# Directional scans as four 48x48 products in the quarters of TensorE's array instead of one 96x96 product

## The chip, the cores and the metric

The kernel runs on one core of a Trainium2 chip. The metric is the device time of one execution in microseconds. All data are fp32.

## The reference, cut to what matters

The input `x` is (4, 48, 256, 256): 4 images, 48 channels. Four layers each add to `x` a function of its group norm (16 groups of 3 channels). Layers 0 and 3 are gated feed-forward layers (1x1 convolution, 3x3 depthwise convolution, GELU gate, 8x8 block DFT with a mask). Layers 1 and 2 are the subject here: four scans over lines, each a recurrence whose step is a convolution of width 5 along the line, from 48 to 48 channels.

```python
def step(w, b):
    def f(carry, inp):
        nxt = inp + _conv1d(carry, w, b)      # 48 -> 48 channels, 5 taps along the line
        return (nxt, nxt)
    return f
# down: rows 0..255;  up: rows 255..0, input shifted by one row, same weights
# right: columns 0..255 of the result of up;  left: columns 255..0
x = x + _L1_conv_ref(_gn(x), ...)
```

A scan has 255 dependent steps. Within one step, the four images and the 256 positions of the line are independent.

## The kernel before, in words

**Stages.** `net_kernel` runs, in this order: `input_stats` (reads `x`, statistics for the first norm), `layer0`, the scans of layers 1 and 2 (`open_scans`, `scans`), `layer3`. Images are taken in two pairs `p`; layers 0 and 3 walk through strips of `RB` = 8 rows, with a hand-written order on TensorE, VectorE and ScalarE (`by_clocks`, `in_turns`).

**A scan step.** A line of a pair is a tile slice of 96 partitions: partitions 0 to 47 hold the even positions of the line, 48 to 95 the odd ones. The free dimension holds 2 images x 128 positions with a zero at each end. In this parity layout the 5 taps over 256 positions become 3 taps over 128 position pairs, with 96x96 weights in which two of the twelve 48x48 blocks are zero (`scan_weights`). `conv` (L728 to L733) issues the three products into one PSUM tile `acc`; then one VectorE instruction adds the incoming line, and the bias where it isn't folded in, and writes the new line (L811 in down, L846 in up, L885 in right, L923 in left). The next product of the pair needs this line.

```python
acc = self.ps1[p].tile([CC, 2, m], F32, name="acc")
for t in range(3):
    self.nc.tensor.matmul(acc, w[:, t, :], carry[:, :, t : t + m], start=(t == 0), stop=(t == 2))
```

**Order.** `scans` runs a generator for each pair. It takes a step of pair 0, then one of pair 1, by turns; pair 1 starts 16 steps later. TensorE and VectorE execute in the order in which the program emits (`manual_schedule`); the other engines and DMA queues are ordered by the scheduler. PSUM gives each pair two buffers of `acc`.

**Around a step**, for each group of 8 lines of a pair:

- *down*: SP loads `in` from the layer's input (L786, L795); two ScalarE ACTIVATEs (L806) apply the norm and the bias in place; after 8 steps Pool issues the write of the lines to `dn` (L818).
- *up*: SP loads `in` from `dn`; ScalarE copies the finished lines, transposed, to `blk` (L853); every fourth group a 32-row block goes to `up` (L858).
- *right*: SP loads `in` from `up`; Pool issues the write to `rt` (L889).
- *left*: SP loads `in` from `rt` (L906); every fourth group ScalarE's queue loads the residual block `blk` from the layer's input (L911), into one of three buffers that both pairs share. After a group, Pool adds the lines to the block in two instructions (L933), VectorE takes `bn_stats` of it during the second half of the next group (L946, four instructions), and the block is written to `xout` (L939).

`in` has three buffers a pair, the lines have three sets of 8. DRAM tensors between the layers keep parity and position in separate dimensions, so a load of 8 lines of `x` or `up` has contiguous runs of 4 x 16 elements, 256 B.

**Layers 0 and 3** read and write that layout too. In layer 0, `back` adds the residual in eight VectorE instructions per half strip (L463) and stores `xo` (L475). In layer 3, `normed` makes `u` from `raw` in eight ScalarE instructions per strip (L1056).

Of the kernel before, what the change touches and what calls it, by code (L numbers as in the profile page):

```python
# [9 lines left out]
F32 = mybir.dt.float32  # L10
AF = mybir.ActivationFunctionType
# [10 lines left out]
BK = 32  # L22
PW = 16
BH = BK // 2
# [7 lines left out]
class Net:  # L32
# [9 lines left out]
    def __init__(self, ctx, tc, args, out, B, H, W):  # L42
# [9 lines left out]
        self.xs = [  # L52
            dram.tile([n, C, 2, 2, self.WB, 2, H // 2, BH], F32, name=f"x{i}", tag=f"x{i}")
            for i in (1, 2, 3)
        ]
        self.dn = dram.tile([n, CC, H, W], F32, name="dn", tag="dn")
        self.up = dram.tile([n, C, 2, 2, self.HB, 2, W // 2, BH], F32, name="up", tag="up")
        self.rt = dram.tile([n, CC, W, H], F32, name="rt", tag="rt")
# [3 lines left out]
        self.grp6 = self.load("grp6", [CC, CC])  # L62


        self.inv1 = self.load("inv1", [128, 64])
        self.fwd1_p = self.load("fwd1_p", [128, 64])

        self.fwd1 = self.load("fwd1", [128, 64])
        self.inv1_p = self.load("inv1_p", [128, 64])
# [11 lines left out]
    def new_stats(self, halves=False, rows=CC):  # L81


        n = self.B if halves else self.NP
        t = self.stat.tile([CP, n, self.NP * self.NCH // n, 6], F32, name=f"st{n}", tag="st")
        return [t[0:rows, p] for p in range(n)]

    def norm(self, stats):
        grp = self.grp if len(stats) == self.NP else self.grp6
        steps = self.norm_steps(stats, self.grp7 if stats[0].shape[0] == CP else grp)  # L90
        while True:
            try:
                next(steps)
            except StopIteration as end:
                return end.value

    def norm_steps(self, stats, grp, name=""):

        nc, n, rows = self.nc, len(stats), stats[0].shape[0]
        with self.tc.tile_pool(name="ps_n", bufs=1, space=PSUM) as psn:  # L100
# [4 lines left out]
            for p in range(n):  # L105
                nc.vector.bn_aggr(mv[:, p, :], stats[p])
                yield
            pm = psn.tile([rows, n], F32, name="pm")
# [21 lines left out]
        return [sc[:, p] for p in range(n)]  # L130

    def by_image(self, scs):

        found = []
        for p in range(self.NP):
            for b in range(2):
                t = self.stat.tile([CC, 2], F32, name=f"si{p}{b}", tag=f"si{p}{b}")
                for k in range(2):
                    self.nc.sync.dma_start(t[k * C : (k + 1) * C, :], scs[p][64 * b : 64 * b + C, :])
                found.append(t)  # L140
        return found

    def strip(self, x, p, lo, hi):

        return x[p].rearrange("c i e v f h w -> i c e (v f) h w")[:, :, :, :, lo:hi, :]
# [17 lines left out]
    def layer0(self, scs, stats):  # L163
# [7 lines left out]
        with ExitStack() as st:  # L171
# [263 lines left out]
            def back(n, z, q0):  # L435
# [6 lines left out]
                if q0 == 0:  # L442
                    state["xo"] = io.tile([CP, 2, self.WB, 2, RH, 2, 8], F32, name="xo", tag="xo")
                xo = state["xo"]
                for q0 in (q0,):
                    po = ps.tile([128, 2, 4, 2, 2, RH, 2, 4], F32, name="po", tag="w")
                    for q in range(4):
                        for l in range(2):
                            for lo, m in ((0, 64), (64, C)):
                                for o in range(2):  # L450
                                    f = slice(64 * o, 64 * o + 64)
                                    nc.tensor.matmul(
                                        po[lo : lo + m, o, q, :, :, :, l, :].rearrange("p e f h w -> p (e f h) w"),
                                        z[f, q0 // 2 + q, l, lo : lo + m], self.inv1_p[f, :],
                                        start=True, stop=True,
                                    )
                    rs = res[:, :, q0 * PW : (q0 + 8) * PW].rearrange(
                        "p (h e) (q w f) -> p e f q h w", e=2, f=2, q=8
                    )
                    for e in range(2):  # L460
                        for f in range(2):
                            for o in range(2):
                                nc.vector.tensor_tensor(  # L463
                                    xo[:, e, q0 // 2 : q0 // 2 + 4, f, :, o],
                                    po[0:CP, o, :, e, f].rearrange("p q h l w -> p q h (l w)"),
                                    rs[:, e, f, o::2], ALU.add,
                                )
                if q0 + 8 < NQ:
                    return
                flat = xo.rearrange("p e v f h l w -> p (e v f h l w)")  # L470
                for k in range(RB * W // MM):
                    nc.vector.bn_stats(stats[p][:, h0 * W // MM + k, :], flat[:, k * MM : (k + 1) * MM])
                to = self.strip(self.xs[0], p, h0 // 2, h0 // 2 + RH)
                for b in range(2):
                    nc.gpsimd.dma_start(  # L475
                        to[b].rearrange("c e v h w -> c (e v) (h w)"),
                        xo[64 * b : 64 * b + C].rearrange("p e v f h l w -> p (e v f) (h l w)"),
                    )
# [210 lines left out]
    def scan_weights(self, n, which):  # L689


        nc = self.nc
        w = self.wp1.tile([CC, 3, CC], F32, name=f"w{n}_{which}", tag=f"w_{which}")
        b = self.wp1.tile([CC, 1], F32, name=f"b{n}_{which}", tag=f"b_{which}")
        nc.gpsimd.memset(w, 0.0)
        taps = self.a[f"L{n}_{which}_w"]
        for e in range(2):
            for f in range(2):
                lo, hi = (1 if e < f else 0), (2 if e > f else 3)
                for t in range(lo, hi):  # L700
                    nc.sync.dma_start(
                        w[e * C : (e + 1) * C, t, f * C : (f + 1) * C], taps[:, 2 * t + e - f, :]
                    )
            nc.sync.dma_start(b[e * C : (e + 1) * C, :], self.a[f"L{n}_{which}_b"])
        self.scan_w[n, which] = w, b

    def open_scans(self, st):

        pool = lambda name, bufs, **k: st.enter_context(self.tc.tile_pool(name=name, bufs=bufs, **k))
        self.wp1, self.pin, self.pblk = pool("w1", 1), pool("in1", 3), pool("blk1", 3)
        self.ps1 = [pool(f"ps1_{p}", 2, space=PSUM) for p in range(self.NP)]
        self.lines, self.turn, self.scan_w = [], [0] * self.NP, {}
        for which in ("down", "right", "left"):
            self.scan_weights(1, which)
        M = self.W // 2
        assert self.H == self.W
        for p in range(self.NP):
            self.lines.append([])  # L720
            for k in range(3):
                t = self.wp1.tile([CC, RB, 2, M + 2], F32, name=f"line{p}{k}", tag=f"line{p}{k}")
                self.nc.gpsimd.memset(t[:, :, :, 0:1], 0.0)
                self.nc.gpsimd.memset(t[:, :, :, M + 1 : M + 2], 0.0)
                self.lines[p].append(t)

    def conv(self, p, w, carry):

        m = self.W // 2
        acc = self.ps1[p].tile([CC, 2, m], F32, name="acc")  # L730
        for t in range(3):
            self.nc.tensor.matmul(acc, w[:, t, :], carry[:, :, t : t + m], start=(t == 0), stop=(t == 2))  # L732
        return acc  # L733

    def scans(self, scs):


        stats = self.new_stats(halves=True)

        def pair(p, scs):  # L740
            for n in (1, 2):
                got = stats[2 * p : 2 * p + 2]
                yield from self.scan_layer(n, p, self.xs[n - 1][p], self.xs[n][p], scs, got)
                if n == 1:
                    if p == self.NP - 1:
                        self.scan_weights(2, "left")
                    scs = yield from self.norm_steps(got, self.grp6, f"p{p}")

        with self.tc.manual_schedule(engines={mybir.EngineType.PE, mybir.EngineType.DVE}):
            going, count = [pair(p, scs[2 * p : 2 * p + 2]) for p in range(self.NP)], 0  # L750
# [7 lines left out]
    def scan_layer(self, n, p, x, xout, scs, stats):  # L758

        nc, W, H, HB, WB = self.nc, self.W, self.H, self.HB, self.WB  # L760
        M, RH = W // 2, RB // 2
        own = lambda pl, p, shape, name: pl.tile(shape, F32, name=f"{name}{p}", tag=f"{name}{p}")
        half = lambda t, e: t[e * C : (e + 1) * C]
        blocks = lambda ap: ap.rearrange("p i (v w) -> p i v w", w=BH)
        inner = lambda ap: ap[..., 1 : M + 1]

# [4 lines left out]


        (wd, bd), shift = self.scan_w[n, "down"], []
        for i in range(2):
            t = own(self.wp1, 2 * p + i, [CC, 1], "shift")
            nc.vector.tensor_tensor(t, scs[i][:, 1:2], bd, ALU.add)
            shift.append(t)
        carry = None
        for h0 in range(0, H, RB):
            ln, _, _ = next_lines()  # L780

            t = own(self.pin, p, [CC, 2, 2, WB, RH, BH], "in")
            for f in range(2):
# [40 lines left out]
        for h0 in range(H - RB, -1, -RB):  # L824
# [12 lines left out]
            if (h0 + RB) % BK == 0:  # L837
                blk = own(self.pblk, 0, [CC, 2, 2, M, BH], "blk")
# [662 lines left out]
```

## Time and profile before

| | |
|---|---|
| median of 3 runs | 13,404.22 us (13,392.09 to 13,425.06) |
| span of the profiled execution, first to last instruction | 13,427.3 us |
| time of that execution around its span | not given separately |
| input statistics | 0 to 336 us |
| layer 0 | 336 to about 3,075 us |
| scans of layers 1 and 2 | about 3,110 to 8,740 us |
| layer 3 | to the end |
| mean granted TensorE clock | 0.971 |
| DMA packets, bytes | 1,170,327; 1,224 MB |

How to read the page: it gives each engine's busy time (TensorE's products as PE, its weight loads as PEld, VectorE as DVE, ScalarE as ACT, GpSimd as POOL), then the span in 40 slices of 336 us with the busy share in tenths, then the DMA queues, then groups of instructions by source line. Of a group it shows busy time in us, the mean duration of one in ns, and after the second bar the idle time ahead of the group's instructions with what ended it. [...] products that follow each other overlap and their durations don't add up; the distance between starts is what a product costs in a stream. In a timeline each line is a start and a length in us, an engine, a source line and an operation, and the number of instructions merged into it.

### The profile page before, as it was taken

What the parts mean: (1) busy time and instruction counts of PE and PEld (TensorE: products, weight loads), DVE (VectorE), ACT (ScalarE), POOL (GpSimd) and SP (SyncE); (2) the same over time, 40 slices, a digit from 0 to 9 for tenths busy, and PEclk for the clock granted to TensorE, in tenths of its full rate; (3) what the DMA queues carried; (4) which work ended last, traced back from release to release, by engine and by line L of the source; (5) the groups of instructions that cost most, each with busy time, mean ns of one, the idle gap of its engine ahead of it and who ended that gap; (6) DMA issues with size and microseconds to landing.
All of it is one profiled execution on the core that took longest, in us unless ns stands there. A gap on an engine that the chain in (4) does not pass through costs nothing.

```text
span 13427.3 us, 418750 instructions
## 1 busy us (share of the span) xinstructions
PE 12419.8 (92%) x195144; PEld 7348.8 (55%) x195144; DVE 7184.5 (54%) x11691; ACT 3956.8 (29%) x4845; POOL 1336.4 (10%) x977
## 2 busy tenths in 40 slices
PE   2999899998999899999998999799999999999999
PEld 1333333335777677767776777544444454444444
DVE  6777777773333334543333346555555555555555
ACT  1444444442223100012231000044444344444443
POOL 0110010100000003520000025300000000000000
PEclk9999999998999999999999999899999999999999
DMA  7222222225755877977658769501011010011010
GB/s 171 56 56 56 57 54 56 57 49 110 154 138 151 169 151 161 229 165 152 138 154 166 154 147 227 133 19 27 22 27 27 22 28 20 22 27 27 22 27 20
DMA packets 1170327, 1224.12 MB, mean 91 GB/s; under 512 B 1027669, under 2 KB 1031757, under 8 KB 1107725
## 3 DMA queue, kind: packets, MB, share of 16 engines
q1 hardware_dynamic: 1070476, 649.55, 24.8%
q0 software_dynamic: 87488, 445.55, 11.5%
q10 hardware_dynamic: 10624, 102.24, 4.4%
q8 instruction: 1532, 25.10, 0.8%
q14 instruction: 207, 1.69, 0.1%
HBM read 699.76 MB, written 497.42 MB: 89 GB/s over the span
## 4 chain that ended last, share of the span: by engine, by line
PE 47%; ACT 4%; DVE 3%; issue 2%; DMA 0%; SPq 0%; POOL 0%; ACTq 0%; DVEq 0%; POOLq 0%
PE acc L732 20%; PE pd L1160 11%; PE pz L1102 4%; PE pp L1139 4%; PE pd L1176 4%; PE po L1256 2%; ACT u L1056 2%; PE pf L1085 1%; DVE g_b L1187 1%; PE pt L1068 1%; PE po L1246 1%; DVE z L1104 1%; ACT z_a L1148 1%; ACT gl L1186 1%; DVE acc L1220 1%
## 5 line engine op out<-in xcount | busy, mean ns | idle before, releaser
L732 PE MATMUL acc<-line,w_down 96*96 96x256 f32 x12240 | 2692.9, 382 | 52.8 <-ACT line L802 31.5
L732 PEld LDWEIGHTS acc<-line,w_down 96*96 96x96 f32 x12240 | 2008.2, 164 | 729.9 <-DVE line L811 34.2
L1160 PE MATMUL pd<-z_a,diag 32*32 32x512 f32 x37152 | 1862.3, 606 | 45.1 <-issue 31.1
L308 PE MATMUL pd<-main,diag 32*32 32x512 f32 x36864 | 1432.8, 623 | 80.0 <-issue 76.4
L1220 DVE SCALAR_TENSOR_TENSOR acc<-z_b,wd,acc 128x1024 f32<-128x1024 f32 (+1 forms) x1056 | 1328.7, 1260 | 307.0 <-ACT acc L1217 275.0
L732 PE MATMUL acc<-line,w_right 96*96 96x256 f32 x6120 | 1339.4, 379 | 82.0 <-DVE line L882 60.0
L732 PE MATMUL acc<-line,w_left 96*96 96x256 f32 x6120 | 1362.5, 384 | 31.2 <-DVE line L923 31.2
L345 DVE SCALAR_TENSOR_TENSOR acc<-rest,wd,acc 128x1024 f32<-128x1024 f32 x1024 | 1256.7, 1284 | 125.7 <-ACT acc L339 125.4
L732 PEld LDWEIGHTS acc<-line,w_right 96*96 96x96 f32 x6120 | 999.0, 163 | 412.0 <-DVE line L882 61.3
L732 PEld LDWEIGHTS acc<-line,w_left 96*96 96x96 f32 x6120 | 1007.8, 165 | 377.5 <-DVE line L923 47.1
L1176 PE MATMUL pd<-z_b,diag 32*32 32x512 f32 x18432 | 1068.5, 604 | 33.8 <-DVE z L1108 22.0
L1104 DVE TENSOR_TENSOR z<-pz,mask 128x512 f32<-128x512 f32 x1024 | 701.6, 685 | 482.0 <-PE pz L1102 477.4
L811 DVE TENSOR_TENSOR line<-acc,in 96x256 f32<-96x256 f32 x1020 | 429.2, 421 | 961.7 <-PE acc L732 951.6
L308 PEld LDWEIGHTS pd<-main,diag 32*32 32x32 f32 x36864 | 504.7, 105 | 795.6 <-issue 681.0
L885 DVE SCALAR_TENSOR_TENSOR line<-acc,b_right,in 96x256 f32<-96x256 f32 x1020 | 489.4, 480 | 834.9 <-PE acc L732 834.1
L1160 PEld LDWEIGHTS pd<-z_a,diag 32*32 32x32 f32 x37152 | 594.0, 103 | 596.4 <-issue 437.9
L846 DVE SCALAR_TENSOR_TENSOR line<-acc,b_down,in 96x256 f32<-96x256 f32 x992 | 476.0, 480 | 810.8 <-PE acc L732 810.8
L120 ACT ACTIVATE nrm<-nrm 96x2 f32<-96x2 f32 (+2 forms) x5 | 1.0, 203 | 2987.7 <-DVE nrm L119 2987.7
L1139 PEld LDWEIGHTS pp<-c_inv,z 64*64 64x64 f32 x36864 | 603.5, 136 | 465.9 <-issue 262.9
L1139 PE MATMUL pp<-c_inv,z 64*64 64x64 f32 x36864 | 676.1, 222 | 171.7 <-DVE g_b L1187 82.6
L923 DVE SCALAR_TENSOR_TENSOR line<-acc,b_left,in 96x256 f32<-96x256 f32 x992 | 475.8, 480 | 563.8 <-PE acc L732 563.8
L933 POOL TENSOR_TENSOR blk<-blk,line 96x1024 f32<-96x1024 f32 x248 | 705.3, 2872 | 644.0 <-DVE line L923 644.0
(158 smaller groups left out, 12383.8 us busy)
## 6 DMA issues: line engine op xcount, KB each, us to landing
blk<-x ACTq DMA_DIRECT2D x64, 1536.0 KB, 20.2
in<-x SPq DMA_DIRECT2D x248, 384.0 KB, 11.1
dn<-line POOLq DMA_DIRECT2D x124, 768.0 KB, 9.3
rt<-line POOLq DMA_DIRECT2D x124, 768.0 KB, 9.5
in<-rt SPq DMA_DIRECT2D x124, 768.0 KB, 12.6
in<-dn SPq DMA_DIRECT2D x120, 768.0 KB, 5.8
in<-up SPq DMA_DIRECT2D x240, 384.0 KB, 9.9
up<-blk POOLq DMA_DIRECT2D x56, 1536.0 KB, 14.3
```

The costliest lines, as they stand in the source:

```text
L308: nc.tensor.matmul(pd[32 * j : 32 * j + 32, i], diag[s, t, :], z[s, R2 * j + t // 3 : R2 * j + t // 3 + R2, t % 3 : t % 3 + W], start=(t = ...
L345: nc.vector.scalar_tensor_tensor(to, at(t, r), wd[:, 1, t : t + 1], to, ALU.mult, ALU.add)
L732: self.nc.tensor.matmul(acc, w[:, t, :], carry[:, :, t : t + m], start=(t == 0), stop=(t == 2))
L846: nc.vector.scalar_tensor_tensor(inner(line), acc, bd, new[r], ALU.add, ALU.add)
L885: nc.vector.scalar_tensor_tensor(blocks(inner(line)), blocks(acc), br, new, ALU.add, ALU.add)
L933: (nc.vector if w0 == 0 else nc.gpsimd).tensor_tensor(part, part, inner(ln[:, f::2])[..., lo:hi].rearrange("p w i h -> p i h w"), ALU.add)
L1102: nc.tensor.matmul(pz[:, b, 0 : 2 * HD], xf[s, q, :], wi[s, :], start=True, stop=True)
L1104: nc.vector.tensor_tensor(z[:, q, 0 : 2 * n].rearrange("p (b c) -> p b c", b=2), pz[:, :, 0:n], mask[:, :, 0:n].to_broadcast([128, 2, n]), ...
L1139: nc.tensor.matmul(pp[to, l, q1, :], z[f, q0 + q, k * NM + 64 * c : k * NM + 64 * c + 64], self.inv1[f, :], start=True, stop=True,)
L1160: nc.tensor.matmul(pd[32 * j : 32 * j + 32, i, 0:n, :], diag[s, 2 if g == "m" else half, t, :], zt[g][s, R2 * j + t // 3 : R2 * j + t // 3 ...
L1176: nc.tensor.matmul(pd[to, i], diag[s, half, t, :], zt[f"b{half}"][s, R2 * j + t // 3 : R2 * j + t // 3 + R2, t % 3 : t % 3 + W], start=(t ...
L1220: nc.vector.scalar_tensor_tensor(made[0], at(t), wd[:, half, t : t + 1], made[0], ALU.mult, ALU.add)
```

## The change

The scans leave the parity layout. Images or half-lines lie on partitions 0 to 47 and 64 to 111 (`CP` = 112 rows, rows 48 to 63 unused and zeroed once), and lines come in two kinds that alternate from step to step:

- kind `a`: partition half = image, free = the 256 positions of the line and two zeros at each end;
- kind `h`: partition half = half of the line, free = 2 images x 130 positions (`HP`: half a line and two positions of the other half) and two zeros at each end.

A product with contraction half `of` and output half `to` lies in one 64x64 quarter of TensorE's array. From a line of kind `a`, the contraction half selects the image and the output half selects the half-line, so the result is of kind `h`; from kind `h` it is the other way round. `conv` issues 5 taps x 4 quarters. `acc` takes two PSUM banks, one for each contraction half, and each pair has one buffer of it instead of two.

```diff
     def conv(self, p, w, carry):
         m = self.W // 2
-        acc = self.ps1[p].tile([CC, 2, m], F32, name="acc")
-        for t in range(3):
-            self.nc.tensor.matmul(acc, w[:, t, :], carry[:, :, t : t + m], start=(t == 0), stop=(t == 2))
-        return acc
+        acc = self.ps1[p].tile([128, 2, MM], F32, name="acc")
+        half_out = len(carry.shape) == 2
+        n = HP if half_out else m
+        for t in range(NT):
+            for to, k in ((0, 64), (1, C)):
+                for of in range(2):
+                    s = slice(64 * of, 64 * of + C)
+                    if half_out:
+                        x = carry[s, (m - 2) * to + t : (m - 2) * to + t + n]
+                    else:
+                        x = carry[s, to, 2 * of + t : 2 * of + t + n]
+                    self.nc.tensor.matmul(
+                        acc[64 * to : 64 * to + k, of, 0:n], w[s, t, 0:k], x, start=(t == 0), stop=(t == NT - 1)
+                    )
+        return acc[0:CP, :, 0:n]
```

The weights are loaded as they are, once for each partition half (two DMAs for a direction's weights instead of ten). `by_image` goes: statistics and norm are kept for a pair on 112 rows.

In down and right, every second incoming line must be brought to kind `h`. `turned`, new, does it on ScalarE with four copies and four small edge copies for each group of 8 lines:

```diff
+        def turned(t):
+            new, e = self.fresh_new[p]().rearrange("p (r i w) -> p r i w", r=R, i=2), M // BK
+            for to in range(2):
+                d = slice(64 * to, 64 * to + C)
+                for i in range(2):
+                    s = slice(64 * i, 64 * i + C)
+                    nc.scalar.copy(
+                        new[d, :, i, 2 * to : 2 * to + M].rearrange("p r (v w) -> p v r w", w=BK),
+                        t[s, e * to : e * to + e, 1::2, :],
+                    )
+                    edge = (slice(M, M + 2), t[s, e, 1::2, 0:2]) if to == 0 else (
+                        slice(0, 2), t[s, e - 1, 1::2, BK - 2 : BK]
+                    )
+                    nc.scalar.copy(new[d, :, i, edge[0]], edge[1])
+            return new
```

`dn` and `rt` become two tensors each, one a kind, so a group is written in two DMAs (`save`) and read in two (`saved`, `halves`). In up, the copies to `blk` are one for the lines of kind `a` and four for those of kind `h`. In left, four ScalarE copies bring the lines of kind `h` to the image layout in `stage` before Pool adds them; Pool still adds in two instructions.

```diff
+            stage = self.fresh_new[p]()[:, 0 : R * W].rearrange("p (r h) -> p r h", r=R)
+            for of in range(2):
+                for i in range(2):
+                    nc.scalar.copy(
+                        stage[64 * i : 64 * i + C, :, M * of : M * of + M],
+                        ln["h"][64 * of : 64 * of + C, :, i, own(of)],
+                    )
```

The tiles `in`, `new` and `blk` are no longer taken from pools. They are rings made once per pair (`ring`), whose rows 32 to 63 Pool zeroes when the scans open: three of 2,064 elements a partition, two of 1,040, two of 4,096; the lines are zeroed on those rows too. A block has 16 columns or rows instead of 32 (`BK`), two blocks to a pair. The residual's load moves from ScalarE's queue to SP's and is issued a block ahead:

```diff
+        def residual(w0):
+            blk = self.fresh_blk[p]()
+            nc.sync.dma_start(blk.rearrange("p h w -> p (h w)"), x[:, w0 // BK].rearrange("c h w -> c (h w)"))
+            return blk
+
+        coming = [residual(W - BK), residual(W - 2 * BK)]
...
             if (w0 + RB) % BK == 0:
-                blk = own(self.pblk, 0, [CC, 2, 2, M, BH], "blk")
-                for e in range(2):
-                    nc.scalar.dma_start(
-                        half(blk, e).rearrange("p i f h w -> p i (f h w)"),
-                        x[:, :, e, w0 // BK].rearrange("c i f h w -> c i (f h w)"),
-                    )
+                blk = coming.pop(0)
+            elif w0 >= BK and w0 + BK < W:
+                coming.append(residual(w0 - BK))
```

The tensors between the layers are now [pair, 112, blocks of 16 columns, rows, 16], so a load of 8 lines has runs of 8 x 16 elements, 512 B, and is one DMA (three for the first group of a direction). Layers 0 and 3 follow this layout with fewer, larger instructions:

```diff
-                    for e in range(2):
-                        for f in range(2):
-                            for o in range(2):
-                                nc.vector.tensor_tensor(
-                                    xo[:, e, q0 // 2 : q0 // 2 + 4, f, :, o],
-                                    po[0:CP, o, :, e, f].rearrange("p q h l w -> p q h (l w)"),
-                                    rs[:, e, f, o::2], ALU.add,
-                                )
+                for o in range(2):
+                    nc.vector.tensor_tensor(
+                        xo[:, q0 + o : q0 + 8 : 2],
+                        po[0:CP, o].rearrange("p q h l w -> p q h (l w)"), rs[:, o], ALU.add,
+                    )
...
-                for e in range(2):
-                    for l in range(4):
-                        nc.scalar.activation(
-                            u[:, l // 2 :: 2, l % 2, e],
-                            raw[0:112, e, :, :, l * 4 : l * 4 + 4].rearrange("p (v f) h w -> p v (f h) w", f=2),
-                            AF.Identity, bias=sc[0:112, 1:2], scale=sc[0:112, 0:1],
-                        )
+                for l in range(2):
+                    nc.scalar.activation(
+                        u[:, :, l], raw[0:112, :, :, l * 8 : l * 8 + 8],
+                        AF.Identity, bias=sc[0:112, 1:2], scale=sc[0:112, 0:1],
+                    )
```

## The prediction, made before the changed kernel was run

> **What bounds the kernel now.** I read the summary lines first, then the costliest groups, then windows inside single scan passes.
>
> ```profile
> PE 12419.8 (92%) x195144; PEld 7348.8 (55%) x195144; DVE 7184.5 (54%) x11691; ACT 3956.8 (29%) x4845; POOL 1336.4 (10%) x977
> ...
> PE   2999899998999899999998999799999999999999
> ...
> L732 PE MATMUL acc<-line,w_down 96*96 96x256 f32 x12240 | 2692.9, 382 | 52.8 <-ACT line L802 31.5
> ...
> L732 PE MATMUL acc<-line,w_right 96*96 96x256 f32 x6120 | 1339.4, 379 | 82.0 <-DVE line L882 60.0
> L732 PE MATMUL acc<-line,w_left 96*96 96x256 f32 x6120 | 1362.5, 384 | 31.2 <-DVE line L923 31.2
> ```
>
> TensorE is the limit nearly everywhere. The scans (3,110 to 8,740 us) hold 24,480 instructions of L732, busy 5,395 us. Down and up take 2,040 steps, right and left 1,020 each: 4,080 steps, so 6 instructions a step (3 products, 2 instructions each).
>
> ```profile
> 3200.00:3640.00 440.00, 440.00 (x2040) 331.76 (x2039) 142.99 (x340) 102.02 (x86) 41.09 (x42) 1.00 0.77 152
> 6550.00:7150.00 600.00, 599.43 (x2778) 451.70 (x2777) 221.87 (x464) 210.91 (x113) 15.01 (x27) 1.00 0.55 146
> 7250.00:7850.00 600.00, 579.25 (x2673) 435.87 (x2672) 214.01 (x447) 4.04 (x4) 54.97 (x57) 0.98 0.80 157
> 7950.00:8500.00 550.00, 550.00 (x2550) 414.73 (x2549) 330.24 (x636) 0.00 (x0) 317.14 (x133) 1.00 0.94 218
> ```
>
> These stretches lie in down, up, right and left; columns: PE, PEld, DVE, ACT, POOL, granted clock, DMA share, GB/s. In the first, 440.00/2,040 = 215.7 ns an instruction, 1,294 ns a step, with no gap. The last two columns are the warning: left, with PE full, has its DMA engines at 0.94.
>
> ```profile
> 5253.86 0.68 DVE L946 BATCH_NORM_STATS2 st<-blk 96x6 f32<-96x512 f32 x1
> 5254.76 0.48 DVE L923 SCALAR_TENSOR_TENSOR line<-acc,b_left,in 96x256 f32<-96x256 f32 x1 [0.21 <-PE acc L732]
> 5255.16 0.68 DVE L946 BATCH_NORM_STATS2 st<-blk 96x6 f32<-96x512 f32 x1
> ```
>
> In left, VectorE's sum and statistics take 1.08 us a step (5254.76 to the statistics' end at 5255.84) in half of the steps.
>
> [...] Layer 3's 64x64 products answer that:
>
> ```profile
> 11033.74 2.08 PE L1085 MATMUL pf<-c_fwd_p,xt 64*64 64x64 f32 x128
> ...
> 11054.17 1.74 PE L1139 MATMUL pp<-c_inv,z 64*64 64x64 f32 x103
> ```
>
> The second stretch less a last product's 0.22 us leaves 1.52/102 = 14.9 ns an instruction, 60 ns for four[...]. So four quarters do run together, loads hidden, also within one row group. [...]
>
> **The change, part by part.**
>
> *Products.* A step becomes 5 taps x 4 quarters x 2 = 40 instructions of 128 or 130 columns, ten deep in each quarter. By scaling 215.7 the price is 10 x 129/256 x 215.7 = 1,087 ns[...]. I take 1,105. Issue isn't the limit: 40 in 1,105 is 27.6 ns apiece, against 14.9 shown. A step saves 189 ns.
>
> *The recurrence.* Two pairs alternate. A pair's own chain is its step (1.105), the lag of the last quarter (six weight loads at 15 ns, 0.09), the drain (382 - 216 = 0.17), and 0.51 to 0.57 around its sum (first steps, one pair alone: 0.51 idle with a 0.42 sum; the sums with bias are 0.48). That is 1.93 us; two steps last 2.21. Cover 0.28 us; were it gone, each missing us lands on every second step. VectorE's 1.08 fits 1.105, barely. One acc buffer a pair instead of two costs nothing: the next product needs that sum's line anyway.
>
> *ScalarE.* It gains turned(): four copies of 48x512 (0.62, L1124's 512-element copy) and four edges (about 0.25) per 8 lines and pair; with one 2,048-element normalisation (2.09, L255) 5.6 us, two pairs 11.2 in the 17.7 us that 16 steps last. Up's copies: 1.94 + 4 x 1 = 6 us, 12 for two. They run a group ahead; queued behind a late one are the other pair's copies, and VectorE's odd lines wait for them. Hidden: 0; uncovered, 3.5 us a group and pair. Left's staging (2.5 us) delays Pool's second sum, where Pool has 8 to 10 us idle between bursts: 0.
>
> *DMA.* Rows go from 96 to 112, half-lines carry 1.6% more. Per group and pair left moved 3 x 768 KB = 2.36 MB, now 2.76: two pairs 5.52 MB in 17.7 us is 311 GB/s.
>
> ```profile
> GB/s 58 0 220 233 145 245 260 175 222 310 149 211 307 164 219 325 179 232 238 180 214 330 158 214 276 179 216 320 172 222 262 175 218 321 161 210 293 184 198 330
> ...
> q10 hardware_dynamic: 2688, 37.75, 39.7%
> q1 hardware_dynamic: 5826, 40.95, 30.6%
> q0 software_dynamic: 2912, 40.90, 23.3%
> ```
>
> Left moved 218 on average with engines 0.94 busy, 330 in its best slices: full engines aren't one ceiling. Bounds: at 330, nothing; at 218, 25 us a group. I take 280: 19.8 us, 1,240 ns a step. The residual load moves from ScalarE's queue to SP's, and its block ring has two 16-column blocks a pair. A load waits there for statistics and for the write of two blocks earlier (15.0 us to land), and the rt loads of both pairs queue behind it: if it blocks, 4 to 9 us per two groups, about 1,310 ns a step; below it, nothing. I count this inside left's 1,240. Down and right go from 152 to 208 GB/s[...]. The fetch queue's engine time per group grows by 7/6 if bytes count, falls to 0.58 if packets do; the share of 17.7 us ends near 0.9. I charge 0.3 us a group, 128 groups: 38 us; bounds 0 and 1.6 us (205). Pool issues two saves instead of one, near 1 us each: hidden, two pairs 4 of 17.7 us.
>
> *Start of scans.* Weight loads, by_image and the split first load cost SP 13.8 + 5.0 + 7.6 us between 3,083 and 3,117; fewer, larger DMAs save perhaps 20. The memsets of new rings (23,000 elements a pair, at 1.8 us per 2,048) delay pair 0 by about 17 us from 3,075, mostly beside that. Gain 10 (bounds -15, +20).
>
> *Layers 0 and 3.* xo: 8 sums (1.67 us) become 2 of about 0.68: VectorE saves 0.3 us x 128, off TensorE's path. u: eight ACTIVATEs, 4.04 us, become two of about 1.2: 1.6 us x 64 = 105 on ScalarE. TensorE idles only 4 to 5 us a step there, mostly for VectorE, so I take 35 together (bounds 0 and 105).
>
> **Sum.** Down, up, right: 3,060 x 189 ns = 578; left: 1,020 x 54 = 55; less 38; plus 10; plus 35: 640 us. The profiled execution's span is 13,427.3 and gives 12,787; no time around the span is shown. It stands 23 us (0.17%) above the median 13,404.2, from which I get 12,764.
>
> **Rivals.** (B) DMA keeps pace throughout: left also saves 189, nothing is charged: 4,080 x 189 = 771 + 45 = 816, so 12,590. For: 330 GB/s slices. Against: 0.94 busy at 218. (C) DMA replaces TensorE: left at 250 GB/s is 22.1 us, 1,380 ns a step, down and right at 19.3 us, 1,206: 1,020 x 189 + 2,040 x 88 - 1,020 x 86 = 285, + 45: 13,075. For: the busy engines and the SP wait. (D) Slower: the weight load of a quarter isn't hidden when its products chain on one accumulator. [...] (column slope of PEld between 103 for 32 and 188 for 128: 0.89 ns, 57)[...], +311 a step: +1,270, less 45: 14,630. It decides for slower beyond about 1,305 ns a step[...]. Against it L1139; for it, that those products don't accumulate. That the quarters don't run at once at all is excluded by the same stretch.
>
> **Chances.** Forecast 0.55, B 0.17, C 0.16, D 0.12. The range runs from below B to above C, 12,500 to 13,120: it takes in 1,087 ns a step with layer 3's larger gain below, and DMA-bound right and left above; it leaves out D. A change within 0.3% (40 us, about what this measurement can tell) would need an accident: 0.02. Faster 0.86, slower 0.12.
>
> **What would show it.** 40 L732 instructions in about 1.1 us a step in up, PE without gaps: products right; 1.6: D. In left, DVE waiting for a DMA, PE for DVE's sum, and groups of over 18 us: how far DMA binds. Gaps behind ACT new: the copies aren't covered. A shorter u with an unchanged layer 3: my 35 is too much. I am wrong if a step outside left misses 1.09 to 1.14, or left is not between 1.1 and 1.38.

## The result, and the profile after

The changed kernel takes 14,825.6 us (median of 4 runs, 14,804.3 to 14,841.1) against 13,398.2 (4 runs, 13,389.3 to 13,425.1): a ratio of 1.1057 with the interval 1.1039 to 1.1075. It is 10.6% slower where 4.8% faster was forecast. The profiled execution's span is 14,839.0 us, 1,411.7 above that of before.

The summary of the page after, with the lines that answer to those of before, and a queue, q8, that the prediction didn't price:

```profile
PE 12564.4 (85%) x333864; PEld 8685.0 (59%) x333864; DVE 7167.9 (48%) x10929; ACT 5177.4 (35%) x7277; POOL 1603.4 (11%) x1197
...
PE   2999999978887887777888778778999999999999
...
PEclk9999999978898888888899788888999999999999
DMA  7222222245555666755555655761000000000000
...
q8 instruction: 2616, 42.86, 1.2%
```

The same queue on the page before:

```profile
q8 instruction: 1532, 25.10, 0.8%
```

TensorE is no longer full in the scans, and no other engine has become full; the granted clock falls in the same slices. Queue q8, which the page calls "instruction", moved 42.86 MB in 2,616 packets: 16 KB a packet, 1,084 packets more. Here and below, "products" counts the MATMUL records of the profile, two for each product that `conv` issues: 40 a step instead of 6. The products of the scans went from 24,480 to 163,200; 138,720/128 = 1,084. In the window of the scans alone (3,081 to 10,051 us) there are 163,200/128 = 1,275 of these packets:

```profile
q8 instruction: 1275, 20.89, 1.3%
```

The whole scans and layer 3 of before, then of after (the last product of the scans of before ends at 8,619 us, not at 8,740 as said above; columns: PE, PEld, DVE, ACT, POOL, granted clock, DMA share, GB/s):

```profile
3113.00:8619.00 5506.00, 5371.57 (x24487) 4017.05 (x24488) 2235.22 (x4646) 784.68 (x527) 1023.57 (x635) 0.98 0.75 162
8619.00:13427.00 4808.00, 4453.19 (x119436) 2272.89 (x119435) 2734.85 (x4060) 1956.42 (x3150) 18.74 (x44) 0.98 0.10 25
```

```profile
3081.00:10051.00 6970.00, 5539.77 (x163207) 5357.71 (x163208) 2265.21 (x4654) 2110.97 (x3345) 1329.24 (x911) 0.85 0.59 153
10051.00:14839.00 4788.00, 4447.55 (x119442) 2270.22 (x119436) 2737.56 (x4059) 1850.57 (x2767) 17.22 (x41) 0.98 0.09 27
```

The scans take 6,970 us instead of 5,506: +1,464, and -52 outside them. Over 4,080 steps that is 1.708 us a step instead of 1.349. The DMA share fell, from 0.75 to 0.59: bandwidth doesn't look like what ran out.

What TensorE waits for in the scans of after, longest in total first (us, times, longest), shows the new wait; in the scans of before the same list has one wait on issue, 19.5 us:

```profile
PE acc L737 <- issue: 1317.2, 587, 6.3
PE acc L737 <- DVE line_h L841: 31.0, 16, 9.7
PE acc L737 <- DVE line_a L936: 26.6, 3, 13.3
```

"Issue" means that no semaphore, engine or DMA of the program held it. The timeline shows where such waits stand (start, duration, group, and in brackets the idle time before it):

```profile
4302.06 2.09 PE L737 MATMUL acc<-line_a,w_down 48*48 48x130 f32 x66 [0.72 <-issue]
4303.90 0.28 PE L737 MATMUL acc<-line_h,w_down 48*64 48x128 f32 x2
4303.95 0.31 PE L737 MATMUL acc<-line_a,w_down 48*48 48x130 f32 x2
4304.01 1.81 PE L737 MATMUL acc<-line_h,w_down 48*64 48x128 f32 x58
4307.73 1.30 PE L737 MATMUL acc<-line_h,w_down 48*48 48x128 f32 x18 [1.91 <-issue]
4308.65 0.43 PE L737 MATMUL acc<-line_a,w_down 48*64 48x130 f32 x2
4308.74 0.50 PE L737 MATMUL acc<-line_h,w_down 48*48 48x128 f32 x2
4308.86 4.50 PE L737 MATMUL acc<-line_a,w_down 48*64 48x130 f32 x76
```

Between the two waits lie 66 + 2 + 2 + 58 = 128 products: with their 128 weight loads, 256 instructions. The second wait comes in the middle of a step (58 products of a row of 76 before it, 18 after), where nothing that the program orders changes. This holds throughout: of the 586 distances from one wait on issue to the next, 580 are multiples of 128 products. The trace's list of single packets shows what ends them: 98% of the waits end 1.20 to 1.77 us after a packet of q8 has landed, while the packets themselves come 4.70 us apart (median).

After the second wait, the 80 products of two steps take 4308.86 to 4312.98, 4.12 us; a little later 80 take 4315.91 to 4318.13, 2.22 us. The granted clock, third from the end of each line, tells the difference; after the first, shorter wait it had not fallen:

```profile
4302.06:4302.80 0.74, 0.74 (x28) 0.74 (x30) 0.00 (x0) 0.00 (x0) 0.00 (x0) 1.00 0.83 310
4308.86:4312.98 4.12, 4.12 (x82) 4.12 (x80) 0.97 (x2) 0.00 (x0) 0.00 (x0) 0.50 0.02 4
```

None of the 217 waits on issue under 1.5 us was followed by the clock of 0.50 in the next 0.5 us; of the 142 from 1.5 to 2.5 us 73 were, and all 38 of over 4.75 us. So a long wait is often followed by a stretch at half speed, a short one never was.

This divides the scans of after. At 1.093 us a step (a tenth of the steps are no longer than 1.094) 4,080 steps are 4,459 us. Waits on issue add 1,317, the other waits of that list 132. The mean granted clock of 0.85 over 6,970 us is a loss of 0.15 x 6,970 = 1,046 (an estimate, with products slowed by the clock as in the two stretches above, 4.12 against 2.22 us); the trace's record of the clock puts 154 of it inside the waits, which are counted already, so 892 are left. The sum is 6,800 of 6,970; the rest is not divided.

**Theory A**, which the experiments test: TensorE needs a packet of 128 products with their loads every 128/40 x 1.093 = 3.50 us; packets don't come faster than about that even on quiet DMA engines, and later while data moves; each late one stops TensorE, and a long stop halves its clock for a while. Against it stand rival D of the prediction (weight loads of a quarter not hidden) and the others that each expectation names with its run.

### The profile page after: what moved, and what is told of

The parts are those of the page before. It is cut to its first block, busy times and chain, and to the rows that moved or that the text cites. A ratio compares the mean times of both kernels' runs of the same rounds, so it can differ in the third digit from the quotient of the medians.

```text
span 14839.0 us, 699017 instructions
## 1 busy us (share of the span) xinstructions
PE 12564.4 (85%) x333864; PEld 8685.0 (59%) x333864; DVE 7167.9 (48%) x10929; ACT 5177.4 (35%) x7277; POOL 1603.4 (11%) x1197
## 3 DMA queue, kind: packets, MB, share of 16 engines
q8 instruction: 2616, 42.86, 1.2%
## 4 chain that ended last, share of the span: by engine, by line
PE 77%; issue 12%; ACT 5%; DVE 3%; DMA 2%; POOL 1%; SPq 0%; ACTq 0%; DVEq 0%; POOLq 0%
PE acc L737 36%; PE pd L1216 11%; PE pd L290 8%; PE pp L1195 4%; PE pd L1232 4%; PE pz L1158 4%; PE po L1312 2%; PE ph L267 2%; DMA gx<-in_x 1%; PE ph L259 1%; PE py L364 1%; PE po L433 1%; PE py L371 1%; PE pf L1141 1%; ACT acc L321 1%
## 5 line engine op out<-in xcount | busy, mean ns | idle before, releaser
L737 PE MATMUL acc<-line_a,w_down 48*64 48x130 f32 (+1 forms) x40960 | 1572.6, 297 | 313.8 <-issue 286.4
L737 PE MATMUL acc<-line_h,w_down 48*48 48x128 f32 (+1 forms) x40640 | 1553.5, 297 | 318.5 <-issue 286.1
L737 PEld LDWEIGHTS acc<-line_a,w_down 48*64 48x64 f32 (+1 forms) x40960 | 1443.5, 141 | 352.4 <-issue 321.7
L737 PEld LDWEIGHTS acc<-line_h,w_down 48*48 48x48 f32 (+1 forms) x40640 | 1430.0, 142 | 358.9 <-issue 328.4
L737 PE MATMUL acc<-line_a,w_right 48*64 48x130 f32 (+1 forms) x20480 | 824.9, 307 | 231.8 <-issue 203.9
L737 PE MATMUL acc<-line_h,w_left 48*64 48x128 f32 (+1 forms) x20480 | 793.5, 296 | 228.3 <-issue 215.9
L737 PE MATMUL acc<-line_a,w_left 48*64 48x130 f32 (+1 forms) x20320 | 833.3, 310 | 168.5 <-issue 157.9
L737 PE MATMUL acc<-line_h,w_right 48*48 48x128 f32 (+1 forms) x20320 | 796.3, 300 | 170.7 <-issue 167.1
L737 PEld LDWEIGHTS acc<-line_a,w_right 48*64 48x64 f32 (+1 forms) x20480 | 751.6, 146 | 251.9 <-issue 222.6
L1195 PEld LDWEIGHTS pp<-c_inv,z 64*64 64x64 f32 x36864 | 606.0, 136 | 459.2 <-issue 327.4
L737 PEld LDWEIGHTS acc<-line_a,w_left 48*64 48x64 f32 (+1 forms) x20320 | 758.5, 148 | 196.3 <-issue 180.7
```

Of the source, the lines that this page charges most:

```text
L737: self.nc.tensor.matmul(acc[64 * to : 64 * to + k, of, 0:n], w[s, t, 0:k], x, start=(t == 0), stop=(t == NT - 1))
L1195: nc.tensor.matmul(pp[to, l, q1, :], z[f, q0 + q, k * NM + 64 * c : k * NM + 64 * c + 64], self.inv1[f, :], start=True, stop=True,)
```

## The experiments

Each kernel ran once with a profile, beside a run of the kernel before on the same chip (13,357 to 13,420). "Scans" is from the first to the last product of the scans, "issue" the wait of the scans' products on issue, both from the traces.

| kernel | products a step | data | time, us | scans | issue |
|---|---|---|---|---|---|
| changed | 40 | all | 14,826 | 6,970 | 1,317 |
| four taps | 32 | all | 14,017 | 6,182 | 824 |
| three taps | 24 | all | 13,125 | 5,281 | 338 |
| saves only | 40 | writes | 13,409 | 5,572 | 488 |
| no traffic | 40 | none | 12,654 | 4,847 | 17 |
| three taps, no traffic | 24 | none | 12,584 | 4,761 | none |
| 26 columns | 40 | none | 12,579 | 4,755 | 34 |
| 26 columns, 16 of the weights | 40 | none | 12,522 | 4,707 | 1,720 |
| 56 rows a transfer | 40 | all | 15,051 | 7,245 | 1,459 |
| 64 and 48 rows | 40 | all | 15,248 | 7,424 | 1,640 |

**No traffic.** All data transfers of the scans are left out, at every place where one is issued:

```diff
-            nc.sync.dma_start(a.rearrange("p r w -> p (r w)"), store["a"][p, :, lo : lo + R, :].rearrange("c r w -> c (r w)"))
...
-                nc.gpsimd.dma_start(store[kind][p, :, at + lo : at + R], b[:, lo:])
+                continue
```

> The changed kernel with all data transfers of the scans left out (loads of in, of the residual and of the saved lines; writes of dn, up, rt and of the layers' outputs); the tiles are zeroed once instead, the scans compute on what lies in them, and layer 3 reads layer 0's output. TensorE's instructions, VectorE's, ScalarE's and Pool's work stay. In the changed kernel TensorE stood still for 1,317 us of the scans' 6,970 with nothing to wait for, always after a multiple of 128 products (256 instructions, one 16 KB packet of the instruction queue), and ran at 1.093 us a step in between. Theory A (instructions come late because their packets share the DMA engines with data): without data the stalls go, the granted clock is 1.00, a step takes 1.10 us, the scans about 4,600 us and the kernel about 12,400. Theory B (the supply of instructions itself doesn't reach 73 per us): the stalls stay, over 1,000 us of them, and the kernel takes over 14,300. Rival C (the waits for data and the DMA load of left decide, stalls are a side effect): left alone becomes faster, down and up don't; about 14,000.

12,653.9 us, 2,172 less than the changed kernel and some 250 more than theory A expected. A window in up (columns as above):

```profile
6101.00:6670.00 569.00, 566.75 (x20134) 555.64 (x20128) 245.47 (x508) 391.08 (x328) 0.00 (x0) 1.00 0.02 5
```

20,134 products in 569 us are 28.3 ns apiece, 1.13 us a step, at full clock and without gaps, with all the copies on ScalarE still there. These products accumulate and load as in the changed kernel, so D is out, and whatever else is to hold a step at 1.7 us must go with the traffic. The waits on issue do (1,317 us against 17), although nothing in the program ties the two. With them goes the loss by a low clock while products ran, 892 us against 100: together 2,092 of the 2,123 us by which the two kernels' scans differ, so little is left for any other way in which traffic could slow the scans. The list of packets also tells where the time goes: a packet of q8 is itself on the way for 1.14 us on average with traffic and 1.05 without, but the median distance from one packet to the next is 4.70 against 3.54. A packet is hardly moved more slowly; it starts later. What keeps it from starting is not shown.

**Fewer products, the same traffic.** Each tap's product covers 216 (or 162) columns and two (or one) of the five taps are left out, so that a step has about the same product time in 24 (or 32) instructions: by the 215.7 ns for 256 columns of before, an estimate, 6 x 182.0 = 1,092 ns (or 8 x 136.5 = 1,092) against 10 x 108.7 = 1,087.

```diff
-        n = HP if half_out else m
-        for t in range(NT):
+        n, nw = HP if half_out else m, 216
+        for t in range(3):
...
+                        x = carry[s, :, t : t + nw // 2]
```

> The changed kernel with 3 taps instead of 5 and 216 columns a product instead of 128 or 130 (two taps are left out, the additional columns are computed and not used): 24 products with their 24 weight loads a step instead of 40[...]. Everything else stays, all transfers too. Theories A and B: a 16 KB packet of instructions now lasts 5.8 us instead of 3.5, so the stalls nearly go; a step of 1.10 us, scans 4,600 to 4,900, kernel 12,400 to 12,800. Rival C (transfers decide): nothing changes, 14,800. Rival D (weight loads of a quarter aren't hidden): 6/10 of their cost goes, about 13,900. Rival E (the clock is halved because quarter products use the array too little): clock stays near 0.85 in the scans, about 14,500. The left pass of this run also shows what the transfers alone allow: 1.24 us a step by the prediction, 1.10 if they keep pace.

> As the run with 3 taps, with 4 taps and 162 columns (one tap is left out): 32 products a step[...]; a packet of instructions lasts 4.4 us. If supply is a rate with a limit (theory B) the stalls fall steeply between 40 and 24 products: some 200 to 500 us left here, kernel 12,900 to 13,400. If it is a latency that data packets lengthen (theory A) they fall about in proportion to how much the packet's 4.4 us exceed the 3.5: the same range, 12,800 to 13,300. Rivals C and E: 14,500 to 14,800.

13,124.6 and 14,016.7 us: in the direction that A expected, but both above A's ranges (12,400 to 12,800 and 12,800 to 13,300), the second by over 700 us. The waits on issue fall with the number of instructions, 1,317, 824, 338, but not to nothing at 24. Three taps moved 236 GB/s in left with a DMA share of 0.84, more than the changed kernel in any pass:

```profile
7660.00:8340.00 680.00, 599.17 (x11612) 539.62 (x11608) 387.63 (x733) 151.03 (x244) 428.18 (x152) 0.91 0.84 236
```

So bandwidth doesn't limit left at 185 GB/s. Rival E is out by the run without traffic, whose 20,134 products in the quarters had a granted clock of 1.00 in up.

**Three taps without traffic** completes a square:

> 24 products of 216 columns a step and no traffic: with the changed kernel, the 24 products with traffic and the 40 without, the fourth of a square. Theory A (few packets or no traffic is enough, each alone): a step of about 1.12 in down, up and right as its products allow, 1.25 to 1.3 in left for Pool's sums, scans 4,700, time 12,450 to 12,600, and no issue waits. If traffic costs by another way than the packets, the 24 products lose to traffic as much as the 40 do: then this one is 2,100 below the run with traffic, near 11,000, which its products alone exclude; so the test is whether the traffic's cost at 24 products (this to 13,125) is far below that at 40 (2,172): expected 550 to 650 against 2,172.

12,583.9. Traffic costs 13,125 - 12,584 = 541 us at 24 products and 14,826 - 12,654 = 2,172 at 40, with the same transfers (expected: 550 to 650 against 2,172). Without traffic, 16 products more a step cost 70. Neither alone costs as much as the two together. So the traffic has no fixed price: what it costs grows with the instructions fetched beside it.

**Only writes.** The loads are left out, lines and blocks are written:

> All loads of the scans are left out (their tiles are zeroed whole), the writes stay: lines of down and right, the blocks of up and left. It leaves about half of the scans' bytes. Theory A: the issue waits fall from 1,317 to about half or less, 300 to 700, and the scans lose about half of their 2,123 us over the run without traffic: 13,700, 13,200 to 14,000. If only loads hold the packets up (another kind of queue): 12,650 to 12,900; if only writes do: 14,500 and more.

13,408.8, inside the range: 37% of the issue wait remains at a DMA share of 0.31 instead of 0.59. Writes and loads both take part.

**The supply by itself.** Without traffic, each of the 40 products covers 26 columns, its own part of the sum, so the taps aren't added:

```diff
+            c = min(26 * t, n - 26)
...
-                        acc[64 * to : 64 * to + k, of, 0:n], w[s, t, 0:k], x, start=(t == 0), stop=(t == NT - 1)
+                        acc[64 * to : 64 * to + k, of, c : c + 26], w[s, t, 0:k], x, start=True, stop=True
```

> The kernel without traffic, and each of the 40 products covers only 26 of the 128 columns (tap t its own 26, so the taps aren't summed): the same number of instructions and sums, a quarter of the product time. Theory A (TensorE takes about one packet of 128 products in 3.5 us and no more): a step stays at 40/128 x 3.5 = 1.09 us, TensorE waits on issue most of the time, the scans stay at 4,700 to 4,900 us and the time at 12,500 to 12,700. Rival G (the products at 107.5 ns each set the pace without traffic, and packets have room): a pair's chain is a step of some 0.3 to 0.6 plus 0.09 + 0.17 + 0.5, two steps, so 0.55 to 0.7 a step, in left 1.1: scans near 2,900 and the time near 10,700.

G's 107.5 ns a product is near half of the 215.7 that 256 columns took before, 107.9. The time is 12,579.1, as A expected, but not for the reason that A gave: there were 34 us of waits on issue, not most of the time, and the clock was 0.50. At half clock the loads of 64 columns could set the same pace (an estimate, from 103 ns a load of 32 columns and 188 of 128 in the trace of before: 0.89 ns a column, 114 ns for 64 at half clock). So the next kernel also loads only 16 columns of the weights and makes only 16 rows of each sum:

```diff
-                        acc[64 * to : 64 * to + k, of, c : c + 26], w[s, t, 0:k], x, start=True, stop=True
+                        acc[64 * to : 64 * to + 16, of, c : c + 26], w[s, t, 0:16], x, start=True, stop=True
```

> As the kernel with products of 26 columns and no traffic, which left two readings open: it ran at half clock (0.50), where a 64-column load at 0.89 ns a column would take 114 ns, and ten in a quarter are 1.14 us a step too. Here only 16 columns of the weights are loaded and multiplied (16 rows of each sum are made, the others stay zero): a load of some 28 ns at half clock, 14 at full, and products of 26 columns, 43 at half, so a slot of some 43 to 71. Theory A (packets of 128 products come no faster than one in about 3.5 us): steps of 1.09 to 1.15 in down, up and right, time 12,400 to 12,650. Rival H (the load at half clock set the pace, packets have room): a pair's chain of about 0.45 to 0.7 + 0.76 in two steps, 0.6 to 0.75 a step and 1.1 in left: scans near 3,000, time near 10,750.

12,521.7, and now the time is spent waiting. The scans' window, the wait, and a stretch of the timeline:

```profile
3058.00:7765.00 4707.00, 2437.24 (x163204) 2016.18 (x163208) 2179.84 (x4654) 2091.36 (x3332) 859.84 (x289) 0.50 0.02 5
```

```profile
PE acc L741 <- issue: 1720.0, 1151, 2.1
```

```profile
3852.63 0.79 PE L741 MATMUL acc<-line_h,w_down 48*16 48x26 f32 x52 [1.48 <-issue]
3853.56 1.05 PE L741 MATMUL acc<-line_a,w_down 48*16 48x26 f32 x76
3856.37 0.23 PE L741 MATMUL acc<-line_a,w_down 48*16 48x26 f32 x2 [1.76 <-issue]
```

52 + 76 = 128 products are done in 1.98 us, and the next come 3856.37 - 3852.63 = 3.74 us after these began. TensorE is busy 2,437 of 4,707 us and still no faster. The scans' 163,200 products are 1,275 packets of 128: 4,707/1,275 = 3.69 us a packet. H is refuted. Without data on the DMA engines, TensorE is fed 128 products in about 3.7 us on average, 1.15 us a step of 40. That average takes in some waits for VectorE; in up and right, where a step took 1.13, it is 3.62 (in up, from 3,700 to 4,200 us, TensorE waits 211 us on issue and 11 on VectorE). The kernel without traffic took the same 1.13 there at full clock, so the pace doesn't seem to hang on TensorE's clock. The changed kernel asks for 3.50: its supply had no slack before any data moved.

**Split transfers.** Every transfer goes as two of 56 rows, and for control as one of 64 and one of 48:

```diff
+        def move(engine, to, of):
+            for lo in range(0, CP, 56):
+                engine.dma_start(to[lo : lo + 56], of[lo : lo + 56])
```

> Every transfer of the scans goes as two of 56 rows. [...] Theory A (instruction packets queue behind data on the 16 DMA engines): [...] the 1,317 us of issue waits mostly vanish and the scans come near the 4,847 us that they take without traffic: 12,650 to 12,900. [...] about 14,600. Rival F (the number of transfers matters, not the engines that they use): slower than 14,826, as the kernel with rows 64 and 48.

> Control for the kernel with 56 rows: as many transfers, of 64 and 48 rows[...]. Theory A: [...] 14,826 or up to 200 more. [...]

15,050.6 and 15,248.5: both slower than the changed kernel, where A expected 12,650 to 12,900 or about 14,600 from 56 rows. The 56 rows are 198 us better than the control, in one pair of single runs. That they leave DMA engines free for the instructions was my assumption; the trace doesn't name the engine of a packet, so it is not shown, and with it A's two figures lose their ground. Twice as many transfers cost 423 us in the control (expected up to 200), so this is no remedy, and rival F was right about the sign.

**Left's other limit.** Without traffic, left still takes 1.30 us a step where up and right take 1.10 (three taps, no traffic). VectorE's statistics wait there for Pool's sums:

```profile
L986 DVE BATCH_NORM_STATS2 st<-blk 112x6 f32<-112x512 f32 x512 | 350.0, 686 | 98.7 <-POOL blk L980 96.7
```

On that kernel, each group's statistics run a group later:

```diff
-            ripe, fresh = fresh, []
+            ripe, older, fresh = older, fresh, []
```

> The kernel of 24 products without traffic, whose left passes take 1.30 us a step against 1.10 in the passes before (0.20 x 1,020 = 204 us); each group's statistics run one group (8 lines of its pair) later, so GpSimd's sums of 3.4 to 3.6 us have long been made. If VectorE's wait for those sums is the loss (its statistics waited 97 us for them, and each such wait holds up the sums behind it): left at 1.13 to 1.17 a step, time 12,420 to 12,460. If it is VectorE's own work, 0.69 of statistics + 0.49 of a sum = 1.18 in half of the steps, and the pair's chain behind it: left stays at 1.25 or more, time 12,540 to 12,584.

12,488.1, 96 less, between the two ranges expected; left falls from 1.304 and 1.299 to 1.174 and 1.187 us a step, and the wait is gone:

```profile
L986 DVE BATCH_NORM_STATS2 st<-blk 112x6 f32<-112x512 f32 x512 | 347.4, 684 | 0.0
```

The wait for Pool was some 0.12 of the 0.20 us. What is left is not VectorE's 0.69 + 0.49 = 1.18: sum and statistics overlap a little, and while they alternate a sum starts every 1.10 us:

```profile
5113.04 0.49 DVE L835 SCALAR_TENSOR_TENSOR line_h<-acc,b_left,in 112x260 f32<-112x260 f32 x1
5113.44 0.68 DVE L986 BATCH_NORM_STATS2 st<-blk 112x6 f32<-112x512 f32 x1
5114.14 0.48 DVE L835 SCALAR_TENSOR_TENSOR line_a<-acc,b_left,in 112x256 f32<-112x256 f32 x1
```

From 4,900 to 5,300 us a step takes 1.10 in left too. The rest lies at the ends: the last 16 steps of the two left passes, in which the second pair finishes, hold 31 of 38 and 38 of 45 us by which the passes exceed 1.10 a step.

Of these kernels, only the two with split transfers compute the whole reference, and both are slower than the changed kernel. None was found that computes it and beats the kernel before.

## Why the prediction was wrong, point by point

**The failed step: "Issue isn't the limit: 40 in 1,105 is 27.6 ns apiece, against 14.9 shown."** The 14.9 came from 103 products of layer 3. This is what the trace of before has next, the quoted line first:

```profile
11054.17 1.74 PE L1139 MATMUL pp<-c_inv,z 64*64 64x64 f32 x103
11056.60 0.58 PE L1139 MATMUL pp<-c_inv,z 64*64 64x64 f32 x25 [0.69 <-issue]
```

The line issues 128 products in a row, 103 + 25, and a wait on issue stands between them. The waits of layer 3 of before name it too:

```profile
PE pp L1139 <- DVE g_b L1187: 82.6, 64, 3.0
PE pp L1139 <- issue: 69.7, 95, 2.3
```

These 103, fewer than the 128 of a packet, ran without a wait on issue; I took their rate for one that lasts. The lasting rate without data traffic, measured later, is 3.62 to 3.69 us for 128, 28.3 to 28.8 ns a product. Against that, 27.6 left no slack at all, and with the scans' traffic 163,200 products in 6,970 us came to 42.7 ns apiece. The 24,480 products of before in 5,506 us (one in 225 ns) asked for far fewer. Nor was going from one packet to the next free: it shows as stops at 128 products with 128 loads and 16 KB a packet on q8, 587 waits and 1,317 us in the scans of after. I had not priced q8 at all.

**The DMA term.** I priced the traffic as bandwidth (left at 1,240 ns a step, 38 us elsewhere); left took about 1,800 ns a step. In left, products waited for issue and VectorE for products; the change's 185 GB/s is below the 236 that three taps moved. The traffic's real price, 14,826 - 12,654 = 2,172 us, is paid through late instructions: the waits on issue and the low clock account for 2,092 of it. Rivals B and C were about bandwidth and neither happened.

**Rival D** came within 200 us of the time (14,630) with the wrong mechanism: its 311 ns more a step, my estimate, asked for 1,294 + 311 = 1,605 ns in every pass, but the fastest tenth ran at 1,094 ns or less, with loads hidden. A near time doesn't confirm a cause. (The traces would have given it 0.89 x 64 = 57 ns for a load and 129/256 x 215.7 = 108.7 for a product, an estimate: 1,657 ns a step and, by the same sum, about 14,840, nearer still, by the same luck.)

**The product price was right**: 1,105 forecast (1,087 by scaling the 215.7 ns of the trace of before, the rest my estimate), 1,093 measured when fed; 189 ns a step would have been saved. As it was, down, up and right took 1.51 to 1.81 us a step on average. Without traffic, the scans take 4,847 us: 659 less than before, against 605 (578 + 55 - 38 + 10) forecast with traffic.

**Left's Pool and statistics** at 0 was wrong for Pool: "VectorE's 1.08 fits 1.105, barely" held (on 112 rows, 5113.04 to the statistics' end at 5114.12 is 1.08 too), but Pool's sums, 3.4 to 3.6 us each on 112 rows, come late. Running the statistics later gained 0.12 us x 1,020 steps = some 122 us of the scans; the loss is hidden in the changed kernel behind the slower supply (there, statistics waited 10 us for Pool).

**ScalarE's copies** at 0 was nearly right: TensorE doesn't wait for ScalarE in the scans of after, and VectorE's sums (L841) waited for `new` (L803) four times, 51.2 us, of which the products' wait on L841 shows 31.0. **Recurrence**: waits on the pair's sums (L841, L843, lines of both kinds) are 66 us, so the cover held where instructions were on time. **Start and layers 0 and 3**: 45 forecast, 32 (start at 3,081 instead of 3,113) + 20 (layer 3) = 52 measured; layer 3's products L1195 waited 138.9 us on issue instead of 69.7.

## What to carry to other kernels

Splitting products into more, smaller ones multiplies instructions: count them against a rate that lasts longer than one packet, not against a short burst, and look at the instruction queue and at "issue" waits in the densest stretch that the kernel already has. Instructions come by DMA too, on q8 here, and their packets came later while data moved (4.70 us from one to the next instead of 3.54, medians), so a dense stream beside heavy traffic paid more than either alone: 2,172 us for the traffic at 40 products a step against 541 at 24. A long stop of TensorE cost twice here: the wait, and the granted clock of 0.50 that followed all 38 waits of over 4.75 us.

## What the runs showed of the hardware

- A packet of 256 instructions (128 products with loads) took 3.62 to 3.69 us on average without other traffic (26 columns, 16 of the weights); 580 of the 586 distances between waits on issue in the changed kernel are multiples of 128 products.
- In the changed kernel, after a wait on issue of under 1.5 us the granted clock was full for the next 0.5 us (217 of 217); after one of over 4.75 us it was at 0.50 (38 of 38).
- The granted clock was 0.50 over the whole scans in both kernels with 26 columns a product, in one of them although TensorE counted as busy for 95% of the time:

```profile
3064.00:7819.00 4755.00, 4502.86 (x163208) 4433.49 (x163208) 2256.00 (x4654) 2099.87 (x3333) 866.68 (x290) 0.50 0.02 5
```

  With 128 columns and the same number of instructions (no traffic) it was 0.97. Which property of the products decides was not tried.
- A product of 96x96 on 256 columns lasted 382 ns in the trace of before, while its like started every 215.7 ns.
- Four products in the four quarters, each accumulating over five taps, ran at 4 x 27.3 = 109 ns a slot in the changed kernel; scaling 215.7 ns gives 108.7 for one product of 129 columns, an estimate. So the four ran together, also the two with the same contraction half, and their loads, 132 to 133 ns each (median), were hidden. The 64x64 products of layer 3 of before, with loads of 136 ns, show the same: 14.9 ns apart, 60 for four, where scaling gives 53.9 for one of 64 columns.
- Twice as many transfers of the same bytes cost the changed kernel 423 us (64 and 48 rows against 112).
